# Gated cross-attention with a router on Trainium2: x turned in 32x32 squares, router product by half chunks, experts chosen in two halves

## The chip, the cores and the metric

The kernel runs on one core of one Trainium2 chip. A core has five engines that run their own instruction queues side by side: TensorE (PE, with its weight loads shown as PEld), VectorE (DVE), ScalarE (ACT), GpSimd (POOL) and SyncE (SP), which here only issues transfers (DMAs). The metric is the device time of one execution in microseconds (us); lower is better.

## The reference, cut to what matters

There are eight sequences b; each has 512 rows (features) of 2048 columns. Everything is float32.

```
xn   = layernorm(x)                       # over the 2048 columns
q, k = Wq @ xn + bq, Wk @ xn + bk         # 256 x 128 for each window of 128 columns
v    = Wv @ ctx + bv
attn = softmax(q^T k / sqrt(32))          # 8 heads, inside each window, masked
x1   = x + tanh(g0) * ((Wo @ gelu(attn v) + bo) * mask)
logits = layernorm(x1) @ router_weight^T + router_bias   # 512 rows x 64 experts, contracted over 2048 columns
w    = softmax(logits), only the 8 largest kept
out  = x1 + tanh(g1) * (layernorm(x1) * sum(w) + w @ expert_bias)
```

So the attention goes along windows of columns, while the router contracts over columns: for the router's product TensorE needs x1 with the columns on the partitions, that is x1 transposed.

## The kernel before

**Chunks and slots.** The 2048 columns of a sequence are cut into 4 chunks of 512 columns (`ch`, 32 over the 8 sequences). Each chunk takes two passes of the main loop, `g = 2*ch` (even) and `g = 2*ch + 1` (odd); a pass is called a slot here. A slot handles two windows of 128 columns. 62 slots run in the loop (from line 852 on), and an epilogue written out by hand does the last two. The loop lets several chunks overlap: slot g makes the scores and the softmax for its own two windows, makes half of the queries and keys (`queries_and_keys`) and half of the values (`values`) of chunk ch+1, weighs the values with the softmax of slot g-1 (`weigh`), applies Wo to chunk ch-1 or ch-2 (`attend`, two of four row blocks in each slot), and does the router's part on chunk ch-2. The order of all instructions of an engine is the order of the calls in the program text (`manual_schedule`); each engine takes its own strictly in that order and waits where an operand or a buffer is not ready.

**The numbers of slots in a sequence.** `fin = g % 8` counts the slots of a sequence. While sequence b is in its slots 0 to 7, the experts of sequence b-1 are chosen, in its slots 2 to 5: mean and rstd of the rows (`aggregate`), the logits gathered (`gather_halves`, `add_halves`, `choose`, `choose_exps`, slot 3), the eight largest kept (`select`, `keep_selected`, slot 4) and turned (`turn_weights`, slot 4). From g = 12 on each slot also finishes a piece of an earlier chunk: `scale_x` on POOL scales two row blocks, `mix` multiplies the expert weights with `expert_bias` on PE (`pb`), adds them on DVE (line 757) and stores the result.

**x transposed on PE.** `turn_x` (line 576) turns 128 columns of chunk ch-2 with four PE transposes into one bank (`px`), and ACT copies it out (line 397). Four such calls in each even slot; `logits` (line 584) multiplies all four row blocks with the router weights at the start of the next odd slot (`pl`), and DVE adds the result to `lgT`.

**The softmax transposed by DVE and DMA.** `turn_blocks` (line 487) has DVE transpose the softmax weights `at` inside 32x32 squares into `blocks` (one buffer), and `move_blocks` (line 497) moves the squares to their place with 16 DMAs of 64 KB. `weigh` of the next slot reads them as `atT`. Between the groups of four moves of an odd slot stand the four loads of the chunk after next (`xn`).

**Queries and keys.** `queries_and_keys` (line 341) makes them in seven half-size products (Strassen's scheme) in four PSUM banks; the results are put together by DVE (seven operations, lines 363 to 381) and POOL (two). Where `between(0)` and `between(1)` are called, other work of the slot is put in, `gelu` among it. On ACT the gelu needs a table load before it and another (with `table_of_exps`) behind it; in a slot 5 ACT then normalises the first chunk of the next sequence (`norm`, line 266), which waits for `aggregate` and `shares_of_mean` on POOL.

**Banks.** PSUM has four banks for scores (`sc0` to `sc3`), two `mm` and two `tr`, each handed on in turn. `values` borrows `sc0`; in slots with a `scale_x` step `attend` of an odd slot borrows `sc1` and `sc2` (`r=m + 1`); `turn_weights` borrows `sc1`. A bank that is borrowed is free when the engine that empties it is done.

Of the kernel before, what the change touches and what calls it, by code (L numbers as in the profile page):

```python
# [22 lines left out]
def flamingo_gated_kernel(  # L23
# [71 lines left out]
    def load_xn(ch):  # L95
        t = work.tile([P, NM, CW], F32, tag="xn", name=f"xn_{ch}")
        xn[ch] = t
        rows = rows_of(x, ch // NCH, columns(ch))
        return [lambda m=m: nc.sync.dma_start(t[:, m, :], rows[:, m, :]) for m in range(NM)]
# [24 lines left out]
    eb_sb = const.tile([2 * E, S], F32, name="eb_sb")  # L124
# [49 lines left out]
    def load_experts():  # L174
        for i in range(2):
            nc.sync.dma_start(eb_sb[i * E : (i + 1) * E, :], eb)
# [121 lines left out]
    def mask(ch):  # L298

        biases[ch] = work.tile([P, CW], F32, tag="bias", name=f"bias_{ch}")  # L300
        nc.vector.tensor_scalar(biases[ch], mks[ch], 0.0, NEG, ALU.is_le, ALU.mult)

    def new_queries_and_keys(ch):
        qss[ch] = work.tile([P, NE, CW], F32, tag="qs", name=f"qs_{ch}")
        kss[ch] = work.tile([P, NE, CW], F32, tag="ks", name=f"ks_{ch}")
# [12 lines left out]
    def first_queries_and_keys():  # L318
# [4 lines left out]
        for m in range(NM):  # L323
            for i, (w, e, pt) in enumerate(parts):
# [6 lines left out]
                if i < NE:  # L331
                    nc.scalar.activation(
                        qss[0][:, e, :], pt, AF.Identity, bias=bq_sb[:, e : e + 1]
                    )
                else:
                    nc.vector.tensor_scalar(
                        kss[0][:, e, :], pt, bk_sb[:, e : e + 1], None, ALU.add
                    )
            yield

    def queries_and_keys(ch, e, between):


        es = slice(e * P, (e + 1) * P)
        x_, t_ = xn[ch], xts[ch]
        q, k = qss[ch][:, e, :], kss[ch][:, e, :]
        bq_, bk_ = bq_sb[:, e : e + 1], bk_sb[:, e : e + 1]
        s5 = work.tile([P, CW // 2], F32, tag="s5", name=f"s5_{ch}_{e}", bufs=1)
        s1, u2, u3, u4 = k[:, c1], q[:, c2], q[:, c1], k[:, c2]
        banks = [product([P, 2, CW // 2], f"qk_{ch}_{e}_0")]  # L350

        def block(i, w_, xb):

            out_ = banks[i // 2][:, i % 2, :]
            for j in range(NM // 2):
                nc.tensor.matmul(  # L356
                    out_, w_[:, j, es], xb[:, j, :], start=(j == 0), stop=(j == NM // 2 - 1)
                )
            return out_

        p1 = block(0, w11, x_[:, d1, c1])
        p6 = block(1, ws2, t_[:, 0, :, :])
        nc.vector.tensor_copy(s1, p1)
        nc.vector.tensor_tensor(u2, p6, s1, ALU.add)  # L364
        banks.append(product([P, 2, CW // 2], f"qk_{ch}_{e}_1"))
        p2 = block(2, w12, x_[:, d2, c1])
        p5 = block(3, ws1, x_[:, d1, c2])
        nc.vector.scalar_tensor_tensor(k[:, c1], p2, bk_, s1, ALU.add, ALU.add)
        nc.vector.tensor_copy(s5, p5)
        nc.gpsimd.tensor_tensor(u4, u2, s5, ALU.add)  # L370
        between(0)
        banks.append(product([P, 2, CW // 2], f"qk_{ch}_{e}_2"))
        p7 = block(4, w21, t_[:, 1, :, :])
        p3 = block(5, ws4, x_[:, d2, c2])
        nc.vector.scalar_tensor_tensor(u3, p7, bq_, u2, ALU.add, ALU.add)
        nc.gpsimd.tensor_tensor(q[:, c2], u3, s5, ALU.add)
        nc.vector.scalar_tensor_tensor(k[:, c2], p3, bk_, u4, ALU.add, ALU.add)
        between(1)
        banks.append(product([P, 2, CW // 2], f"qk_{ch}_{e}_3"))
        p4 = block(6, w22, t_[:, 2, :, :])  # L380
        nc.vector.tensor_tensor(q[:, c1], p4, u3, ALU.add)
# [3 lines left out]
    def values(ch, h, i, r=None):  # L385

        if (ch, h) not in pvs:
            pvs[ch, h] = product([P, NPP, DK], f"pv_{ch}_{h}", r)
# [20 lines left out]
    def scores(g):  # L409
# [5 lines left out]
        for i in range(NPP):  # L415
            ws = slice(h * HW + i * W, h * HW + (i + 1) * W)
            for e in range(NE):
                for r in range(HR):
                    nc.tensor.matmul(  # L419
                        sc[r][:, i, e, :], qss[ch][rows[r], e, ws], kss[ch][rows[r], e, ws],  # L420
# [65 lines left out]

    def turn_blocks(g, i):

        p = pairs[g]
        if i == 0:  # L490
            p["blocks"] = work.tile([P, W // Q, NPP, H, Q], F32, tag="blocks", name=f"blocks_{g}", bufs=1)
        nc.vector.transpose(  # L492
            p["blocks"][:, :, i, :, :].rearrange("p b h j -> p h b j"),
            p["at"][i].rearrange("p h (b j) -> p h b j", j=Q),
        )

    def move_blocks(g, pieces):
# [3 lines left out]
        w = work.tile([P, W // Q, NPP, H, Q], F32, tag="atT", name=f"atT_{g}")  # L501
        for a in range(W // Q):
            for b in range(W // Q):
                nc.sync.dma_start(  # L504
                    w[b * Q : (b + 1) * Q, a, :, :, :], t[a * Q : (a + 1) * Q, b, :, :, :]
                )
            if pieces:
                pieces.pop(0)()
        for i in range(NPP):
            p["atT"][i] = w[:, :, i, :, :].rearrange("p a h q -> p h a q")  # L510
# [31 lines left out]
    x1T, lgT, pos, pls = {}, {}, {}, {}  # L542
# [8 lines left out]
    def attend(ch, m, cs=whole, r=None, engine=None, tag=("x1T", 4)):  # L551
# [24 lines left out]
    def turn_x(ch, k, engine=nc.scalar):  # L576
        px = ps_tr.tile([P, NM, P], F32, tag="tr", name=f"px_{ch}_{k}")
        for m in range(NM):
            nc.tensor.transpose(px[:, m, :], xr[ch][:, m, k * P : (k + 1) * P], ident)  # L579
        t = work.tile([P, NM, P], F32, tag="x1T", name=f"x1T_{ch}_{k}", bufs=4)  # L580
        copy(engine, t, px)
        x1T[ch, k] = t

    def logits(ch, ms=slice(0, NM)):


        pl = product([P, D], f"pl_{ch}_{ms.start}")
        for k in range(KC):
            rows = slice((k % 2) * E, (k % 2 + 1) * E)
            nc.tensor.matmul(  # L590
                pl[rows, ms.start * P : ms.stop * P], rw_sb[:, (ch % NCH) * KC + k, :],
                x1T[ch, k][:, ms, :].rearrange("p m d -> p (m d)"),
                start=(k < 2), stop=(k >= KC - 2),
            )
        if ms.stop == NM:
            for k in range(KC):
                del x1T[ch, k]
        pls[ch] = pl

    def logits_out(ch, ms=slice(0, NM)):  # L600
        b = ch // NCH
        ds = slice(ms.start * P, ms.stop * P)
        pl = pls.pop(ch)[:, ds]
        if ch % NCH == 0:
            lgT[b] = work.tile([P, D], F32, tag="lgT", name=f"lgT_{b}", bufs=1)
            nc.vector.tensor_copy(lgT[b], pl)  # L606
# [20 lines left out]
    def gather_halves(b):  # L627

        pg = ps_tr.tile([P, NM, 2, E], F32, tag="tr", name=f"pg_{b}")
        for m in range(NM):  # L630
            nc.tensor.transpose(
                pg[:, m, :, :].rearrange("p a e -> p (a e)"), lgT[b][:, m * P : (m + 1) * P], ident
# [4 lines left out]
        for m in range(NM):  # L637
            nc.scalar.activation(
                t["halves"][:, m, :, :], pg[:, m, :, :], AF.Copy, scale=t["rs"][:, m : m + 1]
            )  # L640

    def add_halves(b):
        t = experts[b]
        t["lg"] = small.tile([P, NM, E], F32, tag="lg", name=f"lg_{b}", bufs=1)
        v = t["halves"]
        nc.vector.tensor_tensor(t["lg"], v[:, :, 0, :], v[:, :, 1, :], ALU.add)
        nc.vector.tensor_tensor(
            t["lg"], t["lg"], rb_sb[:, None, :].to_broadcast([P, NM, E]), ALU.add
# [83 lines left out]
    def mixed(b, k, stop=True):  # L732
# [3 lines left out]
        for i in range(2):  # L736
            rows = slice(i * E, (i + 1) * E)
            pt = product([P, CW], f"pb_{b}_{k}_{i}")
            nc.tensor.matmul(  # L739
                pt, experts[b]["wT"][rows, mp, :], eb_sb[rows, j * CW : (j + 1) * CW],  # L740
# [48 lines left out]


# [7 lines left out]
    new_queries_and_keys(0)  # L798
# [47 lines left out]

    LAG = 12
# [4 lines left out]
    for g in range(NG - NH):  # L852
# [20 lines left out]
        def turn_x_(k):  # L873
            if xch is not None:
                turn_x(xch, k)


# [5 lines left out]


        scores(g)
        maxima(g, (0, 1))

# [8 lines left out]
        exps(g, 0)  # L896
        exps(g, 1)
        if even and xch is not None:
            attend(xch, 2)
        if lch is not None:  # L900
            logits(lch)
            logits_out(lch)
        maxima(g, (2, 3))
        if even:
            if xch is not None:
                attend(xch, 3)
                del os_[xch], mks[xch]
            if g > 0:
                load_mask(nxt)
        exps(g, 2)  # L910
        exps(g, 3)
        if g > 4:
            read_x(len(over), over)
        divide(g, 0)
        if not even:
# [4 lines left out]

        def between(i):
            if g in (1, 2):
                for k in (2 * i, 2 * i + 1):
                    turn(g1, k)
                    turned(g1, k)
            if fin == 5:
                for m in (2 * i, 2 * i + 1):
                    statistics2(ch - 2, m)
            if i == 0:
                if not even:  # L930
                    mask(nxt)
                divide(g, 1)
                if 1 < g < 5:
                    read_x(len(over), over)
                if fin == 3:
                    gather_halves(b4)
                if fin == 4:
                    select(b4)
                if pch is not None:
                    gelu(pch)  # L940
                    table_of_exps()
            else:
                turn_x_(0)
                if g == 1:
                    read_x(len(over), over)
                if fin == 3:
                    add_halves(b4)
# [294 lines left out]
```

## Time and profile before

| | us |
|---|---|
| median of 3 runs (1236.94 to 1238.47) | 1238.18 |
| the profiled execution | 1242.64 |
| its span, first to last instruction | 1240.9 |
| PE busy | 1209.3 |
| DVE busy | 968.7 |
| ACT busy | 795.8 |
| POOL busy | 792.5 |
| mean granted TensorE clock | 0.996 |

The profiled execution is 1.7 us longer than its span, and 4.5 us above the median. The slots can be read off the timeline of PE by the starts of the scores (`sc`, line 419): the first one starts at 33.0 us, slot 4 at 91.15, slot 12 at 242.07, slot 20 at 389.89, slot 28 at 538.57, slot 36 at 686.21, slot 44 at 834.40, slot 52 at 984.16, slot 60 at 1131.81, slot 61 at 1150.30, and the epilogue at 1165.21. A sequence of eight slots so takes between 147.6 and 149.8 us, 148.3 on average from slot 12 to slot 60. A line of a timeline reads: start, time taken, engine, line, operation, result<-operands, shapes, count, and in brackets the idle time of the engine before it with what ended it. On PE a float32 product shows as two records.

### The profile page before, as it was taken

Reading aid. Unit: us, or ns where it says so; the run is one execution under the profiler, and the core shown is the slowest. Engines: PE = TensorE matmul, PEld = TensorE weight load, DVE = VectorE, ACT = ScalarE, POOL = GpSimd, SP = SyncE. Lnnn points to the kernel's source line nnn. Section 1 sums busy time; section 2 is a strip of 40 time slices with the busy share of each in tenths; the row PEclk is TensorE's granted clock in tenths of the full one; section 3 lists DMA queues with packets and bytes.
Section 4 is the critical chain, followed back from the end, with each engine's and each line's share of the span. In section 5 each row is a group of like instructions: output and inputs, shape, how many; then the busy total and the mean of one; then the engine's idle time right before and its main releaser. Section 6 shows DMA issues by size and latency. Waiting matters only on the chain.

```text
span 1240.9 us, 27273 instructions
## 1 busy us (share of the span) xinstructions
PE 1209.3 (97%) x8572; PEld 840.5 (68%) x8572; DVE 968.7 (78%) x3549; ACT 795.8 (64%) x2717; POOL 792.5 (64%) x817
## 2 busy tenths in 40 slices
PE   8899989999999999999999999999999999999997
PEld 5766767777677677676677667667667667667553
DVE  5677757888778878888878887788877887778776
ACT  2766646767566657657657566667656757656663
POOL 3654655666577665678566677565667666578544
PEclk9999989999999999999999999999999999999999
DMA  8346655666776676676776676676676766565434
GB/s 288 91 133 178 167 166 134 188 194 190 209 232 196 196 223 185 204 225 183 219 224 190 195 228 198 199 221 182 204 230 199 210 188 193 152 196 160 137 121 184
DMA packets 157280, 236.22 MB, mean 190 GB/s; under 512 B 26192, under 2 KB 60496, under 8 KB 157008
## 3 DMA queue, kind: packets, MB, share of 16 engines
q1 hardware_dynamic: 154816, 231.60, 63.5%
q10 hardware_dynamic: 2320, 2.88, 0.7%
q8 instruction: 68, 1.11, 0.4%
q14 instruction: 76, 0.62, 0.2%
HBM read 137.93 MB, written 33.55 MB: 138 GB/s over the span
## 4 chain that ended last, share of the span: by engine, by line
PE 79%; DVE 8%; DMA 5%; ACT 3%; POOL 2%; issue 2%; SPq 1%; DVEq 0%; ACTq 0%; POOLq 0%
PE qk L356 25%; PE po L555 16%; PE pv L391 16%; PE pa L523 5%; PE sc L419 5%; PE pb L739 4%; PE px L579 4%; PE pl L590 3%; DVE at L442 3%; ACT at L454 2%; DMA raw<-in_x 2%; DMA xr<-in_x 1%; SPq L504 1%; DMA mk<-in_mask_Bx1x_ff 1%; DVE st L251 1%
## 5 line engine op out<-in xcount | busy, mean ns | idle before, releaser
L454 ACT ACTIVATE at<-at,nmx 128x128 f32<-128x128 f32 x1024 | 395.1, 388 | 211.6 <-DVE nmx L442 198.2
L463 POOL TENSOR_TENSOR at<-at,rsum 128x1024 f32<-128x1024 f32 x128 | 242.6, 1895 | 263.1 <-DVE rsum L462 263.1
L391 PE MATMUL pv<-wv_sb,cx 128*128 128x256 f32 x1024 | 250.2, 388 | 2.1 <-DMA cx<-in_ctx 2.1
L555 PE MATMUL po<-o,wo_sb 128*128 128x512 f32 x512 | 234.0, 599 | 0.0
L442 DVE CUSTOM_DVE_ANT_0 at<-sc,bias 128x128 f32<-128x128 f32 x1024 | 224.8, 285 | 10.1 <-PE sc L419 10.1
L564 POOL TENSOR_TENSOR xr<-t,xr 128x512 f32<-128x512 f32 x124 | 156.2, 1272 | 101.2 <-DVE t L561 101.0
L391 PEld LDWEIGHTS pv<-wv_sb,cx 128*128 128x128 f32 x1024 | 187.9, 191 | 38.3 <-issue 12.1
L454 ACT ACTIVATION_READ_ACCUMULATOR at<-at,nmx 128x1 f32 x1024 | 191.8, 187 | 0.0
L492 DVE STREAM_TRANSPOSE blocks<-at 128x1024 f32<-128x1024 f32 x120 | 148.0, 1234 | 23.0 <-DMA atT<-blocks 13.3
L555 PEld LDWEIGHTS po<-o,wo_sb 128*128 128x128 f32 x512 | 94.5, 190 | 97.8 <-issue 83.0
L356 PE MATMUL qk<-xt,wq_sb 128*128 128x256 f32 x496 | 128.7, 382 | 6.7 <-DVE qs L364 6.7
L397 ACT COPY x1T<-px 128x512 f32<-128x512 f32 x120 | 69.0, 583 | 99.2 <-PE px L579 98.1
L356 PE MATMUL qk<-xn,wk_sb 128*128 128x256 f32 x496 | 131.4, 387 | 0.5 <-DVE lgT L606 0.3
L356 PE MATMUL qk<-xn,ws 128*128 128x256 f32 x496 | 127.3, 379 | 0.0
L356 PEld LDWEIGHTS qk<-xn,wk_sb 128*128 128x128 f32 x496 | 89.0, 189 | 51.5 <-DVE nmx L442 29.4
L561 DVE SCALAR_TENSOR_TENSOR t<-po,bo_sb,mk 128x512 f32<-128x512 f32 x128 | 94.8, 746 | 34.8 <-PE po L555 34.5
L356 PEld LDWEIGHTS qk<-xt,wq_sb 128*128 128x128 f32 x496 | 89.3, 190 | 22.4 <-DVE qs L364 10.1
L757 DVE TENSOR_TENSOR xr<-pb,xr 128x512 f32<-128x512 f32 x122 | 78.1, 684 | 33.1 <-PE pb L739 32.5
L356 PEld LDWEIGHTS qk<-xn,ws 128*128 128x128 f32 x496 | 94.2, 190 | 12.8
L251 DVE BATCH_NORM_STATS2 st<-raw 128x6 f32<-128x512 f32 x112 | 72.3, 677 | 34.7 <-DMA raw<-in_x 34.4
L419 PEld LDWEIGHTS sc<-ks,qs 32*128 32x128 f32 x2048 | 65.0, 186 | 47.7 <-issue 22.9
L728 POOL TENSOR_SCALAR xr<-xr,xa,xd 128x512 f32<-128x512 f32 x120 | 92.5, 780 | 0.9
(123 smaller groups left out, 1845.6 us busy)
## 6 DMA issues: line engine op xcount, KB each, us to landing
atT<-blocks SPq DMA_DIRECT2D x960, 64.0 KB, 2.5
out_dram<-xr SPq DMA_DIRECT2D x63, 512.0 KB, 5.9
cx<-in_ctx SPq DMA_DIRECT2D x61, 512.0 KB, 7.6
raw<-in_x SPq DMA_DIRECT2D x112, 256.0 KB, 4.9
xn<-in_x SPq DMA_DIRECT2D x112, 256.0 KB, 3.6
xr<-in_x SPq DMA_DIRECT2D x28, 1024.0 KB, 6.1
mk<-in_mask_Bx1x_ff SPq DMA_DIRECT2D x32, 256.0 KB, 7.2
xr<-in_x SPq DMA_DIRECT2D x12, 256.0 KB, 6.7
```

The lines of the kernel that those rows point to most:

```text
L251: nc.vector.bn_stats(st1[b][:, m, piece, :], x_)
L356: nc.tensor.matmul(out_, w_[:, j, es], xb[:, j, :], start=(j == 0), stop=(j == NM // 2 - 1))
L391: nc.tensor.matmul(pv[:, i, :], cx[:, m, i * W : (i + 1) * W], wv_sb[:, m, :], start=(m == 0), stop=(m == NM - 1),)
L419: nc.tensor.matmul(sc[r][:, i, e, :], qss[ch][rows[r], e, ws], kss[ch][rows[r], e, ws], start=True, stop=True,)
L442: nc.vector.tensor_tensor_reduce(p["at"][i][:, e * HR + r, :], p["sc"][r][:, i, e, :], bias, -scale, BIG, ALU.add, ALU.min, p["nmx"][:, r, ...
L454: nc.scalar.activation(at, at, AF.Exp, bias=p["nmx"][:, r, i, e : e + 1], scale=-1.0, accum_out=p["rsum"][:, i, h : h + 1],)
L463: (engine or nc.gpsimd).tensor_tensor(p["at"][i], p["at"][i], rs[:, :, None].to_broadcast([P, H, W]), ALU.mult)
L492: nc.vector.transpose(p["blocks"][:, :, i, :, :].rearrange("p b h j -> p h b j"), p["at"][i].rearrange("p h (b j) -> p h b j", j=Q),)
L555: nc.tensor.matmul(po[:, cs], wo_sb[:, e, m * P : (m + 1) * P], os_[ch][:, e, cs], start=(e == 0), stop=(e == NE - 1),)
L561: nc.vector.scalar_tensor_tensor(t[:, cs], po[:, cs], bo_sb[:, m : m + 1], mks[ch][:, cs], ALU.add, ALU.mult)
L564: (engine or nc.gpsimd).tensor_tensor(xc, t[:, cs], xc, ALU.add)
L728: nc.gpsimd.tensor_scalar(xc, xc, a, d, ALU.mult, ALU.add)
```

## The change

- `turn_x` no longer runs in the loop. `x_in_squares` has DVE transpose two row blocks of x1 of chunk ch-2 inside 32x32 squares into the same `blocks` tile (it grows from 512 to 768 values for each partition and square column), in every slot from 4 on; `move_blocks` moves squares of x and of the softmax in the same 16 DMAs, now of 96 KB. The four `xn` loads are issued ahead of the moves and no longer between them.
- `logits` multiplies half a chunk (two row blocks) in every slot, one slot after its squares were made, into bank `sc3`.
- The experts are chosen in two halves (`up`: row blocks 0 and 1, `low`: 2 and 3). `up` is gathered in slot 3, selected and turned in slot 4; `low` is gathered at the end of slot 4, and chosen, selected and turned in slot 5.
- In `queries_and_keys` ACT takes the two copies `s1` and `s5` from DVE, the third bank is a `tr` bank, and the steps are called one by one from the loop.
- `scale_x` moves from POOL to ACT. `mix` becomes `blended`: `pb` in the `tr` banks, ACT copies them out, POOL adds them.
- In slot 5 `norm` is called ahead of `gelu` (before: behind it). In odd slots `values` uses a `tr` bank and runs both halves ahead of `weigh`.
- `eb_sb` (expert_bias whole, two loads of 512 KB after slot 5) goes; each two slots load 512 columns of it (`load_experts`, 256 KB).

```diff
+    def x_in_squares(g, ch, mp):
+        pairs[g]["x"] = (ch, mp)
+        for i in range(2):
+            t = blocks_of(g)[:, :, AW:].rearrange("p b (k m d) -> p m k b d", m=2, d=Q)
+            nc.vector.transpose(
+                t[:, i, :, :, :],
+                xr[ch][:, 2 * mp + i, :].rearrange("p (k b j) -> p k b j", b=W // Q, j=Q),
+            )
...
+    def blended(b, k):
+        j, mp = k // 2, k % 2
+        mixed(b, k, bank=ps_tr)
+        for i, pt in enumerate(held.pop((b, k))):
+            m = 2 * mp + i
+            xc = xr[b * NCH + j][:, m, :]
+            t = work.tile([P, CW], F32, tag="t", name=f"mixed_{b}_{k}_{i}", bufs=3)
+            nc.scalar.copy(t, pt)
+            nc.gpsimd.tensor_tensor(xc, t, xc, ALU.add)
+        stored(b, k, nc.sync, 0, 2)
...
+            "s1": lambda: nc.scalar.copy(s1, p[1]),
+            "s5": lambda: nc.scalar.copy(s5, p[5]),
```

The odd slots of the loop after the change (even ones from slot 4 on run the same steps with `attend` of chunk ch-2 between the maxima):

```
            maxima(g, (0, 1, 2))
            exps(g, 0)
            do["A"]()
            do["s1"]()
            do["u2"]()
            exps(g, 1)
            maxima(g, (3,))
            if fin == 5:
                add_halves(b4, low)
                choose(b4, low)
                choose_exps(b4, low)
...
            do["B"]()
            do["k1"]()
            do["s5"]()
            do["u4"]()
            exps(g, 2)
            exps(g, 3)
...
            if g % SPB == 5 and b1 < B:
                ln1[b1] = aggregate(st1.pop(b1), S // 512, f"1_{b1}")
                shares_of_mean(b1)
            if not even:
                mask(nxt)
            if fin == 5:
                select(b4, low)
                keep_selected(b4, low)
            do["C"]()
            do["u3"]()
            do["q2"]()
            do["k2"]()
            if lch is not None:
                x_statistics((2, 3))
            divide(g, 0)
            divide(g, 1)
...
            if not even and normed is not None:
                norm(normed)
            if pch is not None:
                gelu(pch)
                table_of_exps()
            do["D"]()
...
        for k in steps:
            scale_x(mb, k, engine=nc.scalar)
...
            for c_, h_ in vals:
                for i in range(NPP):
                    values(c_, h_, i, "tr" if g > 2 else 0 if g > 1 else None)
                values_out(c_, h_)
            if known is not None:
                logits(*known, r=3)
                logits_out(*known)
            if fin == 5:
                turn_weights(b4, (1,))
            weigh_last()
            if fin == 3:
                gather_halves(b4, up)
                add_halves(b4, up)
                choose(b4, up)
                choose_exps(b4, up)
...
            for m in (0, 1):
                attend(pch, m, r=m + 1 if steps else None)
...
        for k in steps:
            blended(mb, k)
```

`turn_weights` itself is unchanged: it puts its transposes into bank `sc1` and ACT copies them out (`wT`).

## The prediction

> **What bounds the kernel now.** I read the chain that ended last first (page, part 4), then busy time in two neighbouring slots, then the one place where PE stood still.
>
> ```profile
> PE 79%; DVE 8%; DMA 5%; ACT 3%; POOL 2%; issue 2%; SPq 1%; DVEq 0%; ACTq 0%; POOLq 0%
> ```
> ```profile
> 612.51:649.14 36.63, 36.63 (x266) 25.68 (x264) 28.96 (x104) 23.73 (x81) 23.39 (x21) 1.00 0.71 210
> ```
>
> The second line holds an even and an odd slot: length, then busy time of PE, PEld, DVE, ACT, POOL, the granted clock, the DMA share. PE works 36.63 of 36.63 us; the others have 8 to 13 us to spare. So a steady slot is as long as its PE work, and only two things matter: what leaves PE, and whether another engine becomes late for PE.
>
> **What leaves PE.** Four transposes of `px` take 0.44 us of PE (the timeline has a `px` at 622.35 and the next work at 622.78), a chunk's sixteen 1.75. They go for 29 of 31 chunks: -50.7. The product `pl` of a whole chunk takes 1.87 (148.09 to 149.96). Eight records of 0.43 that overlap in pairs are 1.74; the 0.13 above that will be paid twice: 29 x 0.13 = +3.8. A pair of slots becomes 36.63 - 1.75 + 0.13 = 35.0, a slot 17.5. If nothing else were late, that is -46.9.
>
> **What the other engines get.** ACT: -67 (116 `px` copies of 0.58), +47 (124 copies `s1`, `s5`; no row has ACT copy 128x256 out of PSUM; between `wT` 128x128, 0.37, and 128x512, 0.58; I take 0.38, as ACT's copies start 0.49 apart at full width), +80 (100 scalings at 0.80), +58 (100 copies `mixed` at 0.58): 914. DVE: -50 (`s1`, `s5`), -64 (100 `xr` additions spaced 0.64), +72 (116 square transposes at 0.62, half of the 1.23 that a transpose of twice the size takes; between 0.62 and 1.23), +4 for half-width `lgT`: 931. Even at 1.23 the squares would leave DVE at 1003. POOL: -78 (scalings at 0.78), +127 (100 additions at 1.27): 842. All stay below 85% of 1190. On average PE would stay the bound; the order inside a slot decides.
>
> I followed the order slot by slot, t from the start of the scores. In ordinary slots everything is in time. Even: `k2` frees the `tr` bank for `pb` at t = 14, needed at 16.3. Odd: the gelu ends at 10.9 and `wo` starts at 12.9; the copy `vT` ends at 14.1, `pb` needs its bank at 16.4. Moves: blocks turned at 13.6, 16 issues spaced 0.605, landing 2.5 (96 KB instead of 64: 2.7, between the rows of 64 KB and 256 KB): 26.0, read 17.5 + 10.9 = 28.4. SP issues 23 or 24 transfers of 0.6 in a slot, 14 of 17.5 us; the four `xn` loads, now ahead of the moves, go out between t = 9 and 11.6, when the blocks (13.6) are not turned yet, so they cost nothing; if the blocks were ready they would put the moves 2.4 later, which is the slack. One `eb` load in two slots adds 0.3 to a slot of SP. Three slots of a sequence are not ordinary.
>
> **Slot 5: ACT comes too late for PE.** These are ACT and POOL in a slot 5 of before (scores from 704.70):
>
> ```profile
> 712.25 0.38 ACT L454 ACTIVATE at<-at,nmx 128x128 f32<-128x128 f32 x1
> 712.74 1.28 ACT L549 ACT_TABLE_LOAD   x1
> 714.04 1.33 ACT L549 ACTIVATE o<-o,bv_sb 128x512 f32<-128x512 f32 x2
> 715.39 1.28 ACT L216 ACT_TABLE_LOAD   x1
> 716.68 0.20 ACT L216 ACTIVATE spare<-half 128x1 f32<-128x1 f32 x1
> 716.79 2.92 ACT L272 ACTIVATE xn<-xn,nmr,rs 128x512 f32<-128x512 f32 x4
> 719.61 0.56 ACT L397 COPY o<-pa 128x512 f32<-128x512 f32 x1
> 720.08 0.57 ACT L397 COPY vT<-pv 128x512 f32<-128x512 f32 x1
> ```
> ```profile
> 712.37 0.22 POOL L236 TENSOR_SCALAR v<-mv 128x4 f32<-128x4 f32 x1
> ...
> 715.41 0.20 POOL L264 TENSOR_TENSOR nmr<-nmean,rs 128x4 f32<-128x4 f32 x1
> ```
>
> The gelu is early, so `wo` is never late. After the change ACT's queue in this slot is: first exp at t = 1.2, sixteen exps 6.17 (706.46 to 712.63), `s1` and `s5` 0.76, two `choose_exps` 0.67 (two rows of 0.33 in slot 3), `norm` 2.92, table 1.28, gelu 1.33, table 1.28 and spare 0.11, two scalings 1.47 (they start 0.73 apart, like `norm`'s four), `vT` 0.49, `wT` 0.37: 18.0. Two waits come in. `choose_exps` stands behind twelve maxima (0.21 apart), `u2`, four maxima and three operations on `lg` on DVE, until 5.75, where ACT is free at 4.65: 1.1. `norm` needs `nmr`, which stands on POOL behind `u4` (which needs `s5`) and takes 3.25 (712.37 to 715.61): 10.9 instead of 9.9: 1.0. `wT` ends at about 20.2.
>
> PE needs it earlier: `turn_weights` puts `pw` in bank `sc1`, and the first `po` takes the same bank. PE reaches that `po` after scores 1.10, `qk` 6.05, `pv` 3.66, `pl` 1.0, `pw` 0.25, `pa` 1.01: t = 13.1. Stall: 7.1 us (4.9 with neither wait and the shortest copies, 9 with both doubled). Behind `po` stand `pb` and the next scores, so the whole kernel waits. In before this slot cost 0.2.
>
> Such a stall costs more than itself:
>
> ```profile
> 158.20:163.00 4.80, 0.00 (x0) 0.02 (x1) 0.01 (x1) 1.23 (x2) 4.72 (x5) 0.86 0.43 105
> 163.00:168.40 5.40, 5.39 (x40) 4.36 (x41) 3.96 (x5) 0.58 (x1) 0.57 (x1) 0.50 0.77 220
> 168.40:172.00 3.60, 3.60 (x11) 1.35 (x9) 0.75 (x1) 0.58 (x1) 0.79 (x1) 0.99 0.55 156
> ```
> ```profile
> 163.01 1.94 PE L523 MATMUL pa<-atT,vT 128*32 128x128 f32 x32 [4.83 <-DMA atT<-blocks]
> 164.88 3.75 PE L391 MATMUL pv<-wv_sb,cx 128*128 128x256 f32 x8
> ```
>
> After 4.8 us of idle PE the granted clock is 0.50 for 5.4 us: `pa` and `pv` take twice their usual 1.01 and 1.83, a loss of 2.6. A stall of 7 us is longer still; I add 2.6 to each.
> [...]
>
> So a slot 5 loses 9.7. Slots 13, 21, 29, 37, 45, 53 have `norm`. Slot 61 has neither `norm` nor `vT`: `wT` ends at 15.7, PE comes at 9.4: 6.3 + 2.6.
>
> **Slots 3 and 4.** In slot 3 `pg` takes the `tr` bank of `pv`, which ACT empties behind gelu, tables and scalings at 14.1 to 14.3, PE is there at 12.9: 1.4. In slot 4 the second `pb` waits for ACT's copies of `pg`: 0.6. (Both 0 to 3.)
>
> **What else goes.** The idle stretch at 158 us in slot 7 belongs to `eb_sb`: the moves behind its two loads took 16.15 us to issue, otherwise 9.7. `eb_sb` goes, the stall too: slot 7 took 25.0, its neighbours 17.3 to 17.5: -7.5 (0 if the larger moves stall there anyway).
>
> **Sum**, against the profiled span of 1240.9. Slots 12 to 59: a sequence becomes 4 x 35.0 + 0.7 (`pg` and `pw`, as before) + 1.4 + 0.6 + 9.7 = 152.4; it was 148.3: +4.1, six times +24.6. Slots 4 to 11 (150.9): eight times 17.5 less `pb` 1.06 is 131.6, plus 5 for `vT` copies that scores wait for and the late gelu of slot 5: 136.6, -14.3 (with slot 7). Slot 60: 0. Slot 61: scores 1.1, `qk` 6.05, `pl` 1.0, `pw` 0.25, `pa` 1.0, stall 6.3, `po` 3.5, `pb` 1.06, clock 2.6 = 22.9 against 14.9: +8.0. Slots 0 to 3: -2 (a 1.3 us wait for `qs` in slot 1 and 1.0 in slot 3, as `u2` comes ahead of the last maxima). Epilogue: +1 (half a `pl`). Total +17.3, span 1258. The profiled execution stands 4.5 above the median, an offset that I carry over: 1238.2 + 17.3, rounded: **1255 us**.
>
> **Rivals.**
> 1. *PE stays the bound* (faster). If slot 5 costs nothing (for instance ACT's waits vanish and `po` isn't held by `wT`): 1255 - 6 x 9.7 - 8.9 = 1188. The full PE row speaks for it, ACT's queue above against it. This mechanism decides the sign: each microsecond of stall is worth 7 us, and with 2.6 of clock kept the change breaks even at a stall of about 4.7 instead of 7.1. Halfway, a stall of 3.5 that costs no clock: 1255 - 7 x 6.2 = 1212.
> 2. *The moves land late.* The slack is 2.4 us in an even slot's moves. Landing has a median of 2.5 but a longest of 10.1 us, and the moves carry 50% more. Late by 2 us in each of 25 odd slots: 1305. Against it: before had the same slack and PE waited for a move once.
> 3. *The stall stays, the clock loss doesn't* (PE idle too short): 1255 - 7 x 2.6 = 1237, the same as before. Against it stand the clock rows above.
>
> **How the numbers follow.** About 0.2% (2.5 us) is what a measurement can tell. Forecast, 1241 to 1280: 0.62. Rival 3 or a stall around 5, 1225 to 1241: 0.15, split over all three signs. Rival 1 with halfway, 1185 to 1225: 0.14. Rival 2, above 1280: 0.09. The likeliest one's own range is 1241 to 1280; the range that holds 8 in 10 also takes in the case of equal time: 1222 to 1282. Faster 0.22, same 0.07, slower 0.71.
>
> **What would show it.** Right: in slots 13, 21, ... the timeline of PE has a gap of 5 to 9 us ahead of `po`, ended by ACT (`wT`), then a granted clock of 0.5; the ordinary slots are 17.5 us; ACT has `norm` ahead of the gelu there; PE busy without the gaps falls by 47. Wrong: no gap ahead of that `po` (then 1188 to 1212), or `pl` and `pa` of many odd slots waiting for DMA (then 1280 or more), or ordinary slots above 18.

## The result, and the profile after

The changed kernel takes 1404.72 us (median of 4 runs, 1400.49 to 1412.88), the kernel before beside it 1238.33 (4 runs, 1236.94 to 1238.95): ratio 1.135, interval 1.130 to 1.141. It is slower, as forecast, but by 166 us where I said 17; 1404.72 lies far above the range of 1222 to 1282. Its profiled execution took 1402.44 us, span 1400.7, mean granted clock 0.936 (before 0.996).

Busy times came out close to the forecast (ACT 914, DVE 931, POOL 842 predicted). From part 1 of the page after:

```profile
PE 1223.4 (87%) x8340; PEld 836.4 (60%) x8340; DVE 945.6 (68%) x3519; ACT 903.1 (64%) x2932; POOL 842.2 (60%) x845
```

PE lost 232 records of work and is still busy for 14 us more: a matmul at half clock counts as busy for longer (`po` below, 6.64 us instead of 3.6). The waits of PE (what waited for what: us in total, times, longest) show where the time went:

```profile
PE pb L776 <- DMA eb<-in_L_ffn_expert_bias: 80.4, 17, 9.4
PE po L585 <- ACT wT L750: 45.9, 7, 6.9
PE pg L664 <- ACT vT L407: 12.7, 6, 2.1
PE pl L624 <- DMA atT<-blocks: 7.2, 4, 3.6
```

The second and third line were forecast (slots 5 and 3). The first was not: the piece of `expert_bias` comes too late for `pb`. The timeline of PE in an even slot of after (scores from 668.32) and of SP beside it:

```profile
683.52 1.99 PE L401 MATMUL pv<-wv_sb,cx 128*128 128x256 f32 x8
694.42 2.08 PE L776 MATMUL pb<-eb,wT 64*128 64x512 f32 x4 [8.91 <-DMA eb<-in_L_ffn_expert_bias]
696.43 2.09 PE L429 MATMUL sc<-ks,qs 32*128 32x128 f32 x32
```
```profile
665.96 13.57 SPq L532 DMA_DIRECT2D atT<-blocks  x16
681.23 0.42 SPq L105 DMA_DIRECT2D cx<-in_ctx  x1
681.71 0.89 SPq L180 DMA_DIRECT2D eb<-in_L_ffn_expert_bias  x1
682.68 1.39 SPq L110 DMA_DIRECT2D mk<-in_mask_Bx1x_ff  x1
```

The load is called at the start of its slot, but SP comes to it at t = 13.4 us, behind the odd slot's sixteen moves (665.96 to 679.53) and four more transfers. `pb` would need it at 685.5 and starts at 694.42: from issue to use 12.7 us for 256 KB. Before, other transfers of this size landed sooner (the last number is the median in us from the issue to the landing, when all data have arrived):

```profile
xn<-in_x SPq DMA_DIRECT2D x112, 256.0 KB, 3.6
mk<-in_mask_Bx1x_ff SPq DMA_DIRECT2D x32, 256.0 KB, 7.2
```

The windows of the same stretch (length; busy time of PE, PEld, DVE, ACT, POOL; granted clock; share of the 16 DMA engines; GB/s) show how it moved:

```profile
687.00:689.00 2.00, 0.00 (x0) 0.00 (x0) 0.15 (x1) 0.00 (x0) 0.00 (x0) 1.00 1.03 172
691.00:693.00 2.00, 0.00 (x0) 0.00 (x0) 0.00 (x0) 0.00 (x0) 0.00 (x0) 0.50 0.19 58
693.00:695.00 2.00, 0.57 (x2) 0.53 (x4) 0.00 (x0) 0.00 (x0) 0.00 (x0) 0.50 0.13 52
```

Until 689 the share is 1.03. At the end the load is all that moves, and the share is 0.13 at 52 GB/s. That is what two of sixteen engines would make; a window gives the share, not which engines moved. The load's source is `eb[None, ...].to_broadcast([2, E, CW])`, an access pattern that begins with a dimension of 2. Whether the load is slow because of that dimension is the question of section 2 below; the prediction didn't ask it.

Slots 7 and 6 of a sequence take what was forecast for an ordinary slot, 17.5 to 17.6 us (650.80 to 668.32, 806.87 to 824.47); slots 0 to 2 don't (27.4, 18.8 and 21.5 on average from slot 12 on). Slot 5 is as forecast, too: 27.0 us on average, 27.7 here (779.20 to 806.87; forecast 27.2), on PE and ACT:

```profile
791.27 1.08 PE L553 MATMUL pa<-atT,vT 128*32 128x128 f32 x32
799.23 6.64 PE L585 MATMUL po<-o,wo_sb 128*128 128x512 f32 x8 [6.88 <-ACT wT L750]
805.81 1.13 PE L776 MATMUL pb<-eb,wT 64*128 64x512 f32 x4
```
```profile
789.96 2.93 ACT L277 ACTIVATE xn<-xn,nmr,rs 128x512 f32<-128x512 f32 x4 [0.77 <-POOL nmr L269]
792.91 1.28 ACT L579 ACT_TABLE_LOAD   x1
794.20 1.33 ACT L579 ACTIVATE o<-o,bv_sb 128x512 f32<-128x512 f32 x2
795.54 1.28 ACT L221 ACT_TABLE_LOAD   x1
796.84 0.20 ACT L221 ACTIVATE spare<-half 128x1 f32<-128x1 f32 x1
796.94 1.50 ACT L760 ACTIVATE xr<-xr,xd,xa 128x512 f32<-128x512 f32 x2
798.35 0.56 ACT L407 COPY vT<-pv 128x512 f32<-128x512 f32 x1
798.82 0.36 ACT L750 ACTIVATE wT<-pw,tgates 128x128 f32<-128x128 f32 x1
```

`wT` starts at t = 19.6 and `po` behind it, after 6.88 us of idle PE (forecast 7.1); then `po` takes 6.64 us where it usually takes 3.6. This is the slowest of the seven: in slots 13, 21, ..., 61 that `po` takes 5.1 to 6.6 us, 5.85 on average, so 2.2 more than usual.

### The profile page after: what moved, and what is told of

The parts are those of the page before. It is cut to its first block, busy times and chain, and to the rows that moved or that the text cites. A ratio compares the mean times of both kernels' runs of the same rounds, so it can differ in the third digit from the quotient of the medians.

```text
span 1400.7 us, 27089 instructions
## 1 busy us (share of the span) xinstructions
PE 1223.4 (87%) x8340; PEld 836.4 (60%) x8340; DVE 945.6 (68%) x3519; ACT 903.1 (64%) x2932; POOL 842.2 (60%) x845
## 5 line engine op out<-in xcount | busy, mean ns | idle before, releaser
L585 PE MATMUL po<-o,wo_sb 128*128 128x512 f32 x512 | 260.9, 656 | 47.0 <-ACT wT L750 45.9
L836 POOL TENSOR_TENSOR xr<-mixed,xr 128x512 f32<-128x512 f32 x100 | 125.1, 1273 | 210.5 <-ACT mixed L835 210.5
L835 ACT COPY mixed<-pb 128x512 f32<-128x512 f32 x100 | 55.3, 587 | 187.9 <-PE pb L776 154.3
L776 PE MATMUL pb<-eb,wT 64*128 64x512 f32 x256 | 85.5, 715 | 80.4 <-DMA eb<-in_L_ffn_expert_bias 80.4
L381 POOL TENSOR_TENSOR ks<-qs,s 128x256 f32<-128x256 f32 x62 | 45.2, 729 | 159.1 <-ACT s L380 159.1
L429 PE MATMUL sc<-ks,qs 32*128 32x128 f32 x2048 | 89.2, 310 | 4.3 <-ACT vT L407 3.4
L519 DVE STREAM_TRANSPOSE blocks<-xr 128x512 f32<-128x512 f32 x116 | 75.4, 688 | 19.6 <-DMA atT<-blocks 18.3
L760 ACT ACTIVATE xr<-xr,xd,xa 128x512 f32<-128x512 f32 x108 | 81.4, 801 | 7.4 <-POOL xa L735 7.4
L277 ACT ACTIVATE xn<-xn,nmr,rs 128x512 f32<-128x512 f32 x112 | 82.1, 805 | 5.9 <-POOL nmr L269 5.9
L452 DVE DVE_READ_ACCUMULATOR2_ANT nmx<- 128x1 f32 x1024 | 85.0, 83 | 0.0
```

The source lines that it names most:

```text
L277: nc.scalar.activation(xn[ch][:, m, :], source[:, m, :], AF.Identity, bias=nmrs[b][:, m : m + 1], scale=ln1[b][1][:, m : m + 1],)
L429: nc.tensor.matmul(sc[r][:, i, e, :], qss[ch, e][rows[r], ws], kss[ch, e][rows[r], ws], start=True, stop=True,)
L452: nc.vector.tensor_tensor_reduce(p["at"][i][:, e * HR + r, :], p["sc"][r][:, i, e, :], bias, -scale, BIG, ALU.add, ALU.min, p["nmx"][:, r, ...
L585: nc.tensor.matmul(po[:, cs], wo_sb[:, e, m * P : (m + 1) * P], os_[ch][:, e, cs], start=(e == 0), stop=(e == NE - 1),)
L776: nc.tensor.matmul(pt, experts[b]["wT"][rows, mp, :], ebs[j][rows, :], start=True, stop=stop,)
L836: nc.gpsimd.tensor_tensor(xc, t, xc, ALU.add)
```

## The experiments

Each kernel ran beside the kernel before on the same chip, whose median was between 1237.9 and 1241.1; ratios are to it.

The theories with a letter are rival explanations; the quoted expectations give each its range.

**1. Whose is the loss: the load or slot 5?** Theory A: the `eb` load comes too late by its place behind the moves; slot 5 is a second, separate loss. Theory B: the load only uncovers other lateness. Theory C: the load does harm wherever it stands.

One `eb` block is loaded once ahead of slot 12 and used for every piece:

```diff
-        if steps and mk % 2 == 0:
-            load_experts(mk // 2)
+        if g == 9:
+            load_experts(0)
+            for j in range(1, NCH):
+                ebs[j] = ebs[0]
```

> The changed kernel, but one block of 512 columns of expert_bias is loaded once ahead of slot 12 and used for every piece (left out: the other three blocks, so the output mixes the wrong columns). Theory A (PE stands still in even slots because the eb block, issued late in SP's queue and slow to land, is not there for pb): the 80.4 us of waits for eb go, and with them the clock loss behind them (PE busy 1223 against 1162 expected, 61 us, of which some 21 belong to slot 5): 1404 - 80 - 40 = about 1284; slot 5 keeps its gap of 6.9 us ahead of po. Rival B (SP's queue as a whole is too long, eb is only what is late first): the moves of 96 KB are late next, PE waits for atT in pl or pa of many odd slots, 1330 or more.

Measured: 1319.13 us, ratio 1.063 (1.060 to 1.067). Between the two: the loads cost 1404.7 - 1319.1 = 86 us, and 64 us above my sum are left. PE now waits for `wT` (46.5), `pl` for its move 16.8 us in 16 places, `pg` 12.4, the scores 7.7 for `t`.

Each load a slot earlier:

```diff
-        if steps and mk % 2 == 0:
-            load_experts(mk // 2)
+        if not even and g + 1 >= LAG:
+            load_experts((g + 1 - LAG) % SPB // 2)
```

> The changed kernel, each eb block loaded one slot earlier (at the start of the odd slot before its first use; same bytes, same number of loads). Theory A, place of the issue: the load has some 20 us instead of 4 to land, no wait of pb for eb is left, 1284 as without the loads. Rival C (the load is harmful wherever it stands, because it takes some 12 us to land and SP's later issues wait for it): moves become late in the odd slots instead, 1310 to 1360.

Measured: 1395.75, ratio 1.124 (1.120 to 1.128), above both ranges. `pb` no longer waits, but the moves do. Waits of PE, then of SP's queue, in this kernel:

```profile
PE pl L624 <- DMA atT<-blocks: 81.9, 23, 6.1
```
```profile
SPq L532 <- DMA eb<-in_L_ffn_expert_bias: 120.7, 25, 5.8
```

So A is wrong on the place: the lateness went from `pb` to `pl`. By the second line, SP issued moves only when the load had landed, 25 times. (Why a move waits for it, no run shows.)

Slot 5 mended: `norm` and its sums of x go behind the copy `o` on ACT, and `pw` of that slot into bank `sc0`:

```diff
-            if not even and normed is not None:
-                norm(normed)
...
-                turn_weights(b4, (1,))
+                turn_weights(b4, (1,), r=0)
             weigh_last()
+            if normed is not None:
+                norm(normed)
+                for k in range(3):
+                    sums_of_x(nxt + 1, k)
```

> The changed kernel with slot 5 mended and eb as in the change: norm (and the sums that need it) stand behind gelu, scalings, vT, wT and o on ACT, and the second half of the turned weights goes to bank sc0, which odd slots do not use, so po no longer waits for wT. The gap of 6.9 us and the 3.0 us of half clock go in seven slots: 1404 - 69 = 1335 if stalls add up. Theory A says that they do not: in the slot-5 stall SP catches up, which is why slot 6 has no eb wait; with the stall gone slot 6 waits for eb by 5 to 9 us plus the clock: 1360 to 1395.

Measured: 1394.81, ratio 1.124 (1.121 to 1.127), at the upper end of theory A's range. Slot 5 fell to 17.9 us and the wait for `wT` is gone, yet only 10 us of some 60 are saved. Slot 6, with the late `norm` and the late load, now takes 24 to 25 us (17.6 in the changed kernel), and the even slots' waits for `eb` grew from 80.4 to 89.1 us.

Both edits together:

> The eb block one slot earlier and slot 5 mended, together. Theory A with the working of slot 5: 1284 - 69 = about 1215, faster than the kernel before (1238); ordinary slots 17.5 us and few gaps. Rivals B and C (SP's queue too long without any stall to catch up in): 1240 to 1300, with waits for atT or blocks.

Measured: 1383.39, ratio 1.116 (1.113 to 1.119). All expectations missed: `pl` waits 73.1 us for its moves.

**2. Is it the two engines?** Theory D: the load is slow because it runs on two engines, which the share of 0.13 suggests. The same bytes at the same place, in two transfers whose first dimension is 64:

```diff
-        nc.sync.dma_start(t, eb[None, :, j * CW : (j + 1) * CW].to_broadcast([2, E, CW]))
+        for i in range(2):
+            nc.sync.dma_start(t[i * E : (i + 1) * E, :], eb[:, j * CW : (j + 1) * CW])
```

> Changed kernel, with one edit: each eb piece is loaded by two transfers of 64 partitions instead of one that begins with a broadcast dimension of 2. Same bytes, same place in the order. Theory D (the piece is slow because that transfer runs on two of the sixteen DMA engines, and the moves queue behind it there): it lands in less than half of 12 us, pb waits for eb less than 10 us in all (after: 80.4), time 1300 to 1340, as with a single eb load (1319). Theory C (the extra 256 KB in a slot are harmful however they travel): the wait stays above 60 us, time 1370 or more. My prediction's sum was 1255; both expect more, since slot 5 keeps its gap and slots 2 to 4 lost more than predicted in the single-load kernel.

Measured: 1349.78, ratio 1.088 (1.086 to 1.090): 55 us better than the changed kernel, 31 above the single load. As D said, the larger part comes back, though D's range ends at 1340 and its 10 us of waits became 30. Each half lands in 6.2 us (median). The waits of `pb` in this kernel, and a window inside one of 4.8 us, in which no engine computes and all DMA engines are busy (share 1.07 instead of 0.13):

```profile
PE pb L777 <- DMA eb<-in_L_ffn_expert_bias: 30.2, 10, 4.8
844.00:845.00 1.00, 0.00 (x0) 0.00 (x0) 0.00 (x0) 0.00 (x0) 0.00 (x0) 1.00 1.07 218
```

With slot 5 mended as above:

> The kernel before this one, with slot 5 mended as well: norm and its sums of x stand behind o on ACT, pw of that slot is in bank sc0. Theory D: the 7 us gap ahead of po in slot 5 and its half clock go (about 9.7 x 6 + 8.9 = 67 us), slot 6 takes back some of it (it was 22 to 24 us in both earlier kernels with this edit, of which the eb load explains a part): 1235 to 1275. Theory C: 1350 or more, as the earlier kernel with slot 5 mended gained only 10 us. A rival to D's sum: the late norm moves the loss to slot 6, so that the gain against the kernel before is below 20 us.

Measured: 1332.14, ratio 1.075 (1.070 to 1.079): 18 us gained, as the rival to D's sum said. Slot 5 is 17.9 us, slot 6 is 23.8 (936.86 to 960.60).

The part alone in the kernel before: no `eb_sb`, four buffers of 512 columns, a piece in each even slot from slot 12 on, by the transfer with the broadcast:

```diff
+        if steps and mk % 2 == 0:
+            load_experts(mk // 2)
...
-        if g == 5:
-            load_experts()
```

> The kernel before the change, with one part of the change: no resident eb; a piece of 256 KB is loaded at the start of each even slot from slot 12 on, by one transfer that begins with a broadcast dimension of 2 (four buffers, so that the end needs no further load). Theory D: the part alone costs what it costs in the changed kernel (1404.7 - 1319 = 86 us) within a half, less about 5 for slot 7: 1275 to 1340, with pb waiting for eb and moves waiting for it. Rival: the piece only hurts beside the larger moves of 96 KB: below 1250.

Measured: 1376.59, ratio 1.110 (1.106 to 1.113): 137 us for this part alone (25 loads), without any of the change's other parts, and 37 above D's range; the rival is out. `pb` waits 93.6 us for `eb`, 24 times, and a window of a wait shows the share of 0.13 again, at 51 GB/s:

```profile
648.00:650.00 2.00, 0.00 (x0) 0.00 (x0) 0.00 (x0) 0.00 (x0) 0.00 (x0) 0.50 0.13 51
```

The same with two transfers of 64 partitions:

> The same kernel, each piece loaded by two transfers of 64 partitions. Theory D: nearly free, 1232 to 1250 (slot 7 of before loses its 7.5 us stall, 28 pieces of 256 KB come in). Theory C: like the kernel with the broadcast, within 15 us.

Measured: 1287.51, ratio 1.039 (1.034 to 1.043). The spread alone is worth 89 us here. Both theories missed: 47 us are left, with 31.6 us of waits of `pb` for `eb`.

The same, each piece a slot earlier:

> The kernel before with eb pieces by two transfers of 64 partitions, each issued a slot earlier (the last but one kernel of the same kind had them in the slot of their use: 1287.5). Theory D with place: waits of 31.6 and as much again of half clock go, 1232 to 1255. Rival (256 KB more in a pair of slots cost time wherever they stand, with no wait for eb itself): 1270 to 1295.

Measured: 1263.61, ratio 1.019 (1.017 to 1.021). Neither range holds it; no wait for `eb` is left, 23 us are, although slot 7 takes 17.6 us instead of 25.0, as `eb_sb` is gone. The waits that grew are PE's for DVE and DVE's for moves (before 0.4, 0.7 and 13.3 us in all):

```profile
PE pl L593 <- DVE xr L760: 6.6, 8, 1.5
PE sc L422 <- DVE t L564: 5.2, 12, 1.2
DVE blocks L495 <- DMA atT<-blocks: 38.4, 24, 2.7
```

So the pieces probably make the moves late, and these DVE. No run tests this.

**3. The clock term.** In the kernel of section 2 with the spread load (1349.8), 14 matmuls that nobody reads fill the gap of slot 5:

```diff
+            if fin == 5:
+                spare_bank = product([P, CW], f"fill_{g}", 0)
+                for _ in range(14):
+                    nc.tensor.matmul(
+                        spare_bank, ident, wq_sb[:, 0:2, :], start=True, stop=True
+                    )
```

> The changed kernel with eb by two transfers of 64 partitions (1349.8), and in slot 5, ahead of the first po, 14 extra matmuls of 128x512 (about 6.3 us) into an idle bank, whose result nobody reads. They fill most of the 6.9 us in which PE waits for wT, so that PE doesn't stand idle. My step on the clock (a stall of 7 us costs 2.6 us more at half clock): po takes 3.6 us instead of 6.6, 7 x 3.0 = 21 us less: 1322 to 1337. Rival (po is slow for another reason, or the filling only takes time): 1345 to 1360.

Measured: 1369.72, ratio 1.104 (1.101 to 1.108). My filling was mis-sized: a float32 product has two records of 0.44 us, so it took 12.28 us instead of 6.3. But `po` behind it took 3.60 us. At the right length, 7 matmuls:

> As the earlier kernel with the filled gap in slot 5, with 7 matmuls instead of 14 (there each took 0.877 us in two passes, 12.3 us in all, and po behind them 3.6 us instead of 6.6). 7 x 0.877 = 6.1 us of the 6.9 us gap. If the clock loss follows the idle time: po near 3.6, 1325 to 1337 against 1349.8. Rival (a gap of 0.8 us is enough for the loss, or the filling delays ACT): 1345 to 1360.

Measured: 1332.05, ratio 1.077 (1.073 to 1.081), 18 us less than without the filling, at no less work. Timeline of PE in a slot 5 of this kernel:

```profile
594.77 6.28 PE L1120 MATMUL fill<-wq_sb,ident 128*128 128x512 f32 x14
601.75 3.70 PE L586 MATMUL po<-o,wo_sb 128*128 128x512 f32 x8 [0.70 <-ACT wT L751]
```

`po` starts no earlier and takes 3.70 here. In the seven slots it takes 3.6 to 3.7 with the filling, and without it 5.1 to 6.75, 6.1 on average: 17 us in all, against 17.7 measured. So the half clock after the gap is a cost of its own, and it follows the idle time.

**4. What is left?** The changed kernel with all of these mended: the load spread and early, slot 5 as above but with the sums of x between the additions of `po` and those of `mixed` on POOL, and `pg` in a bank of its own:

```diff
-        pg = ps_tr.tile([P, n, 2, E], F32, tag="tr", name=f"pg_{b}_{ms[0]}")
+        pg = product([P, n, 2, E], f"pg_{b}_{ms[0]}", 0 if 0 in ms else 2)
...
+        if not even and normed is not None:
+            for k in range(3):
+                sums_of_x(nxt + 1, k)
         for k in steps:
             blended(mb, k)
```

> The changed kernel with every loss that the runs named mended: eb by two transfers of 64 partitions, issued a slot earlier; in slot 5 pw in bank sc0, norm behind o on ACT and its sums of x on POOL between the additions of po and those of mixed; pg in a bank of its own. From the kernel with eb spread and slot 5 mended (1332): eb waits -35 and some 2 us of half clock for each of twelve (-24); pg -13 and about 1.4 of clock for each of six (-8); slot 6 -4 x 6: about 1230, range 1215 to 1265. Theory D (spread and place are both needed) expects that. Rival: an early load pushes the moves back whatever its spread, as in the earlier kernel with the early load (1396 and 1383): above 1310, with pl waiting for atT.

Measured: 1308.16, ratio 1.055 (1.053 to 1.058): the best complete version of the changed kernel, and still slower than before. Both expectations missed (the rival's bound by 2 us). `pl` waits for moves 37.6 us in 23 places.

Without loads (one block, as in the first experiment):

> The mended kernel (1308) with a single eb block loaded once ahead of slot 12 and used for every piece; the other three blocks of eb are left out, so the output is not the reference's. Theory F (the larger moves are late by themselves: single blocks buffer, transposes 3.8 + issue of sixteen moves 10 to 13 + landing 2.3 is about a slot): 1265 to 1295, pl still waits for atT ten times or more and DVE for moves ahead of the squares. Theory E (all that is left comes from the eb loads): 1215 to 1245, with hardly a wait of pl for atT.

Measured: 1281.81, ratio 1.034 (1.032 to 1.037). So 26 us are the loads', spread and early as they are. The rest isn't: by the prediction's sum a slot 5 that costs nothing gives 1188. The largest piece of that rest, 31 us, is in slot 6, which takes 22.8 us on average and took 17.6 in the changed kernel. Theory F's range holds the 1281.81. Its chain can be seen on DVE in this kernel, which waits for the last move ahead of the next squares because `blocks` is one buffer:

```profile
DVE blocks L519 <- DMA atT<-blocks: 43.6, 24, 4.8
```

Before, DVE waited 13.3 us for moves in all. Squares 1.3, softmax 2 x 1.25, issue of sixteen moves 11.3 (median; 10.0 to 16.2) and landing 2.2 make 17.3 us, a whole slot of 17.5; before it was 2 x 1.23 + 11.3 (626.80 to 638.12) + 2.5 = 16.3 in an even slot of 18.4.

The loads on ACT's queue instead of SP's, in the mended kernel and in the kernel before:

```diff
+        if not even and g + 1 >= LAG:
+            load_experts((g + 1 - LAG) % SPB // 2, queue=nc.scalar)
```

> The mended kernel with the eb loads issued from ACT's queue at the end of the odd slot, not from SP's. Same bytes, same layout. Theory S (the load hurts as one more transfer in SP's queue, whose issues wait for those ahead): within 10 us of the kernel without loads. Theory B (its bytes and packets hurt on the DMA engines): within 10 us of 1308.

Measured: 1306.84, ratio 1.057 (1.053 to 1.061): as on SP (1308.16).

> The kernel before with eb pieces by two transfers of 64 partitions, issued from ACT's queue a slot early (on SP's: 1263.6). Theory S: 1236 to 1250. Theory B: 1256 to 1270.

Measured: 1265.52, ratio 1.022 (1.018 to 1.024): as on SP (1263.61). Theory S's ranges miss twice, B's hold: what is left of the loads is 23 to 28 us from either queue. ACT's queue isn't free, though: in the second kernel ACT waits 30.9 us for loads, in 5 places, and in the first SP's moves still wait 18.0 us for them.

Is F the rest? Three kernels with the single `eb` block, in which `pl` reads x as it stands, so that it waits for no move. The control still moves 96 KB; the second moves 64 KB; the third doesn't make the squares either:

```diff
-        n = AW + XW if "x" in p else AW
+        n = AW
...
-            squares[p["x"]] = w[:, :, AW:].rearrange("p a (k m d) -> p k m a d", m=2, d=Q)
+            c_, m_ = p["x"]
+            squares[c_, m_] = xr[c_][:, 2 * m_ : 2 * m_ + 2, :].rearrange(
+                "p m (k a d) -> p k m a d", a=W // Q, d=Q
+            )
```

> The control: moves of 96 KB as in the mended kernel with one eb block (1281.8), but pl reads x as it stands, so that it doesn't wait for the move (pa, 1 us behind it, still does); the router's product is of an unturned x. Theory F: 1265 to 1283. If only pl's own wait counts: 1245 to 1262, like the kernel without the extra bytes.

Measured: 1288.17, ratio 1.038 (1.035 to 1.041), above both ranges: that `pl` no longer waits for moves (17.1 us with one `eb` block above) gains nothing.

> The mended kernel with one eb block (1281.8), and moves of 64 KB: the squares of x are made on DVE but not moved, pl reads x as it stands (so the router's product is of an unturned x). Theory F (the enlarged moves are late, hold the blocks buffer and through DVE all that stands behind): 1235 to 1262, at least 15 us below the control that moves x without reading it. Theory G (the order of DVE and POOL around po is what is left): within 8 us of the control.

Measured: 1275.38, ratio 1.028 (1.024 to 1.033).

> As the kernel with moves of 64 KB, and the squares of x aren't made either (72 us of DVE work left out). If DVE's added work matters by itself: at least 10 us below that kernel. Theory F: within 8 us of it.

Measured: 1271.21, ratio 1.027 (1.024 to 1.029).

The extra bytes of the moves are worth 13 us, below the 15 that F asked for and above the 8 that G allowed; the squares 4, which the intervals don't separate. F is a part, not the rest. In the third kernel PE waits for what DVE does behind `po`:

```profile
PE sc L429 <- DVE t L594: 18.7, 30, 2.2
PE pg L667 <- DVE lgT L643: 9.4, 7, 1.4
PE qk_B L367 <- DVE t L594: 8.2, 7, 2.5
```

These waits fit theory G, the order of DVE and POOL; no run changes that order by itself, so for what F leaves it is argued and not shown. My own mending of slot 5 brought some of it: slot 6 still takes 22.8 us there (730.72 to 753.49), where the changed kernel took 17.6, six times some 5 us. In it PE waits 2.4 us for `t`, and the clock is 0.93 on average over the slot.

## Why the prediction was wrong, point by point

The miss is 1404.7 - 1255 = 150 us. The single-load kernel divides it: 86 us are the loads, 64 the rest. Its span is 60 us above the 1258 of the sum, and by slots that is 28 (slots 0 to 2), 13 (slot 3), 5 (slot 4) and 14 (slots 0 to 11 of the run).

- **Failed step: "One `eb` load in two slots adds 0.3 to a slot of SP."** I costed the issue and never the landing, nor what is queued behind it. It costs 86 us in the changed kernel and 137 alone in the kernel before. Shown: the form of the load (one transfer that begins with 2 had a share of 0.13; as two that begin with 64, 55 and 89 us come back). Of what is then left in the kernel before, 24 us belong to the place behind the moves, and 23 us stay for pieces that are spread, early and on either queue; the waits of DVE for moves grew there, but how those 23 arise isn't settled. One thing was there to be read: in the kernel before SP issued the odd slot's moves until 621.63, 9.1 us into the even slot that begins at 612.51. What a first dimension of 2 costs, no row of before shows.
- **Slot 5: right.** 7.1 us of stall forecast, 6.88 measured (slot 61: 6.3 and 4.6). For the clock 2.6 us were forecast; `po` took 1.5 to 3.0 us longer in the seven slots, 2.2 on average, and the filling shows that this follows the gap. The slots 5 of the single-load kernel average 27.1, forecast 27.2.
- **Slots 3 and 4: right in kind, too small.** Forecast were 1.4 and 0.6 with no clock term. In the single-load kernel slot 3 takes 21.5 us on average, 2.2 more than my terms and the 0.4 of `pg` itself. The windows of that slot (708 to 718):

```profile
710.66:712.80 2.14, 0.01 (x2) 0.00 (x0) 1.37 (x2) 2.13 (x6) 1.73 (x6) 1.00 0.83 162
714.00:715.00 1.00, 1.00 (x2) 0.33 (x1) 0.97 (x2) 0.00 (x0) 0.92 (x2) 0.50 1.14 353
716.00:717.00 1.00, 1.00 (x3) 0.44 (x2) 1.00 (x3) 0.77 (x4) 1.00 (x2) 0.51 1.07 342
717.00:718.00 1.00, 1.00 (x4) 0.32 (x2) 1.00 (x2) 0.00 (x0) 1.00 (x1) 1.00 1.08 388
```

  After only 2.14 us of idle PE the clock is 0.50 until 717. Not every such gap does this: in the changed kernel one of 2.15 us ahead of the same `pg` leaves it at 1.00.

```profile
1100.65:1102.80 2.15, 0.00 (x2) 0.00 (x1) 1.29 (x2) 2.14 (x6) 1.74 (x6) 1.00 1.04 359
1104.00:1106.00 2.00, 2.00 (x6) 0.89 (x5) 1.93 (x3) 0.00 (x0) 1.92 (x3) 1.00 1.00 267
```

  I added the clock to the long stall and not to the short ones. Stall and clock together are about 13 us more than forecast over six sequences in slots 3, and 5 in slots 4.
- **The moves: rival 2 came true in part.** I gave it 0.09 and a slack of 2.4 us. In the single-load kernel slots 0 to 2 of a sequence take 57.2 us on average instead of 52.5, 28 us over six sequences, with 16 waits of `pl` for moves in the whole run. The moves didn't land later than forecast (median 2.2 us with the spread load, forecast 2.7). The slack had their issue wrong, 9.7 us or sixteen times the spacing inside a group: in the single-load kernel the sixteen took 10.0 to 15.5, 11.2 in the median, and the row of before at 626.80 already has 11.32, which alone makes the slack 0.8. The extra bytes account for 13 us in the control pair; that the rest is order on DVE and POOL is argued from waits.
- **Slots 0 to 11: -16.3 forecast (-2 and -14.3), -3.3 measured.** Slot 12 starts at 238.81 instead of 242.07 (in the single-load kernel at 239.68). The stall of 7.5 us in slot 7 did go (16.5 us instead of 25.0), but slots 0 to 3 lost 4.0 instead of winning 2 (slot 4 starts at 95.18 instead of 91.15), and slots 4 to 11 won 7.3 instead of 14.3.
- **Slots 6 and 7, busy times, slot 61, epilogue without loads: right.** 17.5 and 17.6 in slots 7 and 6; ACT 903, DVE 946, POOL 842; slot 61 22.1 (forecast 22.9); epilogue 76.1 in the single-load kernel (forecast 76.7). With loads it is 87.1 (one wait of 9.15 us for `eb`).
- **Rivals 1 and 3** did not come: the stall stayed, and the clock loss with it. The sign was forecast for the right reason (slot 5 outweighs what PE saves), but slot 5 and slot 61 cost only some 61 us here (45.9 of waits for `wT` and 7 x 2.2 at half clock). The sum had a loss of 17 in all; most of the 166 us came by ways that it did not have.

No kernel here beats the one before. The transposes of `px` do leave PE, but the moves, the pieces of `eb` that make room for them, and ACT's and POOL's new work return more than that in waits and half clock.

## What to carry to other kernels

Cost a new transfer by when it lands and by what stands behind it in the queues, and look at the first dimension of its access pattern as well as at its bytes: 25 loads of 256 KB whose source begins with a dimension of 2 cost 137 us in an otherwise unchanged kernel, and 47 as two transfers each that begin with 64. Where TensorE is the bound engine, a new wait can have two prices, the wait and the half clock behind it, and here even waits of 2.1 us paid the second one, though not all. A mending that only moves a late piece of work moves the stall: look at the slot behind the mended one before counting the gain.

## What the runs showed of the hardware that was not expected

- A transfer whose source begins with a broadcast dimension of 2 had a share of 0.12 to 0.13 of 16 DMA engines, 45 to 52 GB/s, while nothing else moved; one of 256 KB took 12.7 us from issue to use.
- In the single-load kernel the clock fell to 0.50 for about 3.4 us after 2.14 us of idle PE (0.82 on average from 712.80 to 714, 0.50 to 0.51 until 717). In the changed kernel it stayed at 1.00 after 2.15 us, and with 7 matmuls in the gap it was 1.00 behind 0.70 us (601.75 to 605.40). So here a gap of 2.1 us can be enough and need not be.
- Filling the gap of seven slots (6.9 us, in slot 61 less) with 6.3 us of matmuls that nobody reads made a kernel 18 us faster.
- Pieces of 256 KB, spread, early and from either queue, still cost 23 to 28 us over 26 to 28 pieces, about 1 us each, though PE never waited for one. In the kernel before, this is net of the stall in slot 7 that went with `eb_sb`.
